# A second nested product in the setup, and three outer differences made by ScalarE and adding DMAs

## The chip, the cores and the metric

The kernel runs on one core of one Trainium2 chip. The metric is the device time of one execution in microseconds (us). The core has TensorE (PE: matmul, with its weight loads shown apart as PEld), VectorE (DVE), ScalarE (ACT), GpSimd (POOL), and SyncE (SP), which here only issues DMAs. GpSimd issues DMAs too, the ones that add to what stands at their destination. Each engine takes its instructions in order, and waits on semaphores for those of others.

## The reference

All is float32. With x of shape 8 x 1024 x 1024, a context `memory` of 8 x 64 x 512, and D = 1024:

```python
memory_proj = jnp.einsum('bme,de->bmd', memory, W_mem)
scores = jnp.einsum('bnd,bmd->bnm', hidden_states, memory_proj) / jnp.sqrt(jnp.float32(D))
attn = jax.nn.softmax(scores, axis=-1)
memory_context = jnp.einsum('bnm,bmd->bnd', attn, memory_proj)
gate_input = jnp.concatenate([hidden_states, memory_context], axis=-1)
gate = jax.nn.sigmoid(jnp.einsum('bnf,df->bnd', gate_input, W_gate) + b_gate)
fused = hidden_states + gate * memory_context
return _rmsnorm(fused, norm_w)
```

The large part is x times the first half of W_gate, W1 (1024 x 1024), for 8192 rows. The second half, W2, meets the context through attention: the kernel computes `mp`, the projected memory (512 rows of 1024 for all batches), and `mg`, mp times W2, once in a setup, and then only multiplies attention rows with them.

## The kernel before

**Blocks.** x is worked through in 16 blocks of 512 rows. A block's product with W1 is a Strassen product in Winograd's form on two levels: seven outer products (order 1, 6, 7, 5, 4, 2, 3), each of seven inner products of two 128x128 by 128x256 matmul pairs. The outer right sides are W1's quarters or differences of them: `outer_b[5] = 7 - 1` (quarter numbers: 1 upper left, 7 upper right, 2 lower left, 3 lower right), `outer_b[6] = 3 - 5`, `outer_b[7] = 3 - 7` in place, and `outer_b[4] = 2 - 6`. Each is 128 partitions by 2,048 columns. `outer_sum` makes them on VectorE. For each outer product o, four `inner_sum`s (T1, T2, R12 in place, T4; 128x512 each) prepare the inner right sides. `inner_s` does the same for the left sides, from the transposed x, on GpSimd. Before the second outer product of block 0 the scores of block 0 are computed, into the PSUM banks "b" and "c", which the inner products kB and kC of the first outer product have used and which two VectorE adds (u<-u,kB and u<-u,kC) free.

**Setup.** mp is made by Strassen on W_mem. Then mg is made by one outer Strassen level with the quarters m11 to m22 of mp (left) and b11 to b22 of W2 (right): `mg_product` is one dense product of 16 matmul passes of 512 columns; `second_product` replaces one by seven smaller ones (28 passes of 256 columns), with left sums from `second_left` (VectorE) and right sums from `second_right` and `second_sum` (GpSimd). In before only the fifth product (s1 by t1) is nested; the sixth (s2 by t2), like the others, is dense. While TensorE runs through the setup, GpSimd makes W2's and W1's differences, and VectorE makes left sums, outer differences, the transposes of block 0's x (`transpose_x`) and its outer left sums (`outer_s`).

**Order.** The order on every engine is the program's own: `pin` keeps each instruction in the order in which it is written. Buffers are shared by tag: `const` tags t4, t5, t6 hold W1's outer differences 4, 5, 6, and before that W2's t1 (t6) and t2 (t4); it1 to it7 hold the inner sums; it4 first holds the rows of mp that `first_rows` stores. `load_xq(q)` loads a block's x, 2 MB, in four DMAs from SP into the one buffer `xq`, when the transposes of the block ahead are done. After the setup a list of due times (`at`, by slots of one inner product) places the rest of the work between the products.

Of the kernel before, what the change touches and what calls it, by code (L numbers as in the profile page):

```python
# [15 lines left out]
P = 128  # L16
# [4 lines left out]
def tile_gated_cross_attention_rmsnorm(  # L21
# [73 lines left out]
    def tt(eng, o, a, b, op):  # L95
        pin(eng.tensor_tensor(o, a, b, op))  # L96
# [112 lines left out]
    pt += [bank("c", [P, BM], "pt3")]  # L209


    def outer_sum(o, a, b, k=slice(0, 4)):
        tt(nc.vector, outer_b[o][:, k], outer_b[a][:, k], outer_b[b][:, k], ALU.subtract)

    def inner_sum(eng, o, n):
        s, a, b = ((T1, R12, R11), (T2, R22, T1), (R12, R22, R12), (T4, R21, T2))[n]
        tt(eng, w_op(o, s), w_op(o, a), w_op(o, b), ALU.subtract)

    def inner_sums(eng, o):
        w1_place(o)  # L220
        for n in range(4):
            inner_sum(eng, o, n)
# [94 lines left out]
    def w2_sum(eng, o, a, b):  # L317
        for k in range(KH):
            tt(eng, o[k], a[k], b[k], ALU.subtract)

    def second_right(r, tag):
# [4 lines left out]
        return r11, r21, r12, r22, *(t[:, i, :, :] for i in range(3))  # L326

    def second_sum(eng, right, n):
        r11, r21, r12, r22, t4, t1, t2 = right
        o, a, b = ((t1, r12, r11), (t2, r22, t1), (t4, r21, t2), (r12, r22, r12))[n]  # L330
        tt(eng, o, a, b, ALU.subtract)

    right5 = second_right(t_w2[0], "it3")
    for k in range(KH):
        tt(nc.gpsimd if k > 1 else nc.vector, t1[k], b12[k], b11[k], ALU.subtract)
    for n in range(3):
        second_sum(nc.gpsimd, right5, n)
    w2_sum(nc.gpsimd, t2, b22, t1)
    second_sum(nc.gpsimd, right5, 3)
    pm_sum(m22, m22, up)  # L340
    outer_sum(5, 7, 1)
    w2_sum(nc.gpsimd, b12, b22, b12)
    inner_sums(nc.gpsimd, 1)

    pm_product(both, ps4, e22)
    pm_copy(m21, both)
    pm_product(up, pw22, e21)
    pm_copy(m12, up)


    A, S, L2, O = {}, {}, {}, {}
# [4 lines left out]
    def transpose_x(q, t, half):  # L356

        key = q, t // 2, half
        if key not in A:
            A[key] = t4k(  # L360
                apool, [P, KH, 2 * P], f"a{t // 2 + 1}{half + 1}", f"a{t // 2 + 1}{half + 1}_{q}"
            )
        r = t % 2
        pin(
            nc.vector.transpose(  # L365
                A[key][:, :, r * P : (r + 1) * P],
                chunks(xq[q][:, 4 * t : 4 * t + 4, :], KD)[:, half * KH : (half + 1) * KH],
            )
        )
# [167 lines left out]
    def store_mpT(r, h):  # L537
        load(mpd[:, h * KH : (h + 1) * KH, r * HM : (r + 1) * HM], mpT[r][h])
# [22 lines left out]

    def first_rows():

        t = const.tile([P, 2, Q4], F32, tag="it4", name="rows0")
# [22 lines left out]
    def second_left(eng, l, tag):  # L587

        l11, l12, l21, l22 = quarters(l)
        t = const.tile([P, 5, 2, P], F32, tag=tag, name="mg_left")  # L590
        s1, s2, s3, s4, zs = (t[:, i, :, :] for i in range(5))
        tt(eng, s1, l21, l22, ALU.add)
        tt(eng, s2, s1, l11, ALU.subtract)
        tt(eng, s3, l11, l21, ALU.subtract)
        tt(eng, s4, l12, s2, ALU.subtract)
        return l11, l12, l22, s1, s2, s3, s4, zs.rearrange("p k c -> p (k c)")

    def second_product(left, right, pgs, between):

        l11, l12, l22, s1, s2, s3, s4, zs = left  # L600
        r11, r21, r12, r22, t4, t1, t2 = right
        top, low = pgs
        u2 = bank("b", [P, C], "mg_u2")
        z = u3 = bank("c", [P, C], "mg_u3")

        def product(o, l, r, start=False):
            for k in range(2):
                mm(o, l[:, k, :], r[:, k, :], start and k == 0, k == 1)
# [15 lines left out]
        product(top[:, C:H], s4, r22)  # L624
        between()
        product(low[:, 0:C], l22, t4)
        tt(nc.vector, low[:, C:H], low[:, C:H], zs, ALU.add)

    def mg_tile(pool, tag, name):
        return t4k(pool, [P, 2, H], tag, name)  # L630

    def mg_copy(o, pgs):
        for t in range(2):
            pin(nc.scalar.copy(o[t] if isinstance(o, list) else o[:, t, :], pgs[t]))
# [5 lines left out]
        )  # L640

    s1 = mp_step(nc.vector, "s1", apool, m21, m22, ALU.add)
    store_mpT(0, 1)
    load_xq(0)
    c11 = mg_tile(rot, "u", "mg_c11")
    c12 = mg_tile(rot, "u", "mg_c12")
    c21 = mg_tile(rot, "l2", "mg_c21")
    c22 = mg_tile(small, "mg", "mg_c22")
    up, side = side, up
    mg_product(m11, b11, up, True)  # L650
    mg_copy(both, up)
    left5 = second_left(nc.vector, s1, "it6")

    def left6():
        nonlocal s2
        s2 = mp_step(nc.vector, "s2", apool, s1, m11, ALU.subtract)

    s2 = None
    second_product(left5, right5, side, left6)
    mg_copy(c22, side)  # L660
    outer_sum(7, 3, 7)
    w1_place(7)
    for n in range(4):
        inner_sum(nc.gpsimd, 7, n)
    mg_product(m12, b21, up)
    mg_copy(c11, up)
    store_mg(c11, 0, 0)
    first_rows()
    load_mp(0)
    s3 = mp_step(nc.vector, "junk", small, m11, m21, ALU.subtract)  # L670
# [36 lines left out]
    outer_s(0, 2)  # L707
    load_mg(0)


# [484 lines left out]
```

## Time and profile before

| | |
|---|---|
| median of 3 runs | 945.4 us (945.01 to 946.05) |
| the profiled execution's own time | 944.76 us |
| its span, first to last instruction | 943.0 us |
| TensorE busy | 932.1 us (99%) |
| VectorE, GpSimd, ScalarE busy | 801.6, 736.8, 432.5 us |
| granted TensorE clock | 0.997 |
| setup's mg products on TensorE | from 31.5 us to 78.8 us |
| x loads, 512 KB each, issue to landing, median | 9.9 us |
| GpSimd's adding DMAs, 512 KB each, issue to landing, median | 8.3 us |

A row of the timeline gives start, duration, engine, line, operation, output tile <- input tiles, shapes, count, and in brackets the idle time before it with what ended it. Nearly all matmuls go through one helper (line 93) and nearly all two-input sums through another (line 96), so rows are told apart by tile names: t_w is W2's t1 or t2, w a buffer of W1 or W2, t an outer difference, it an inner sum, l inner left sums, mg_u the small PSUM banks of the nested product, pm_af, pm_ed and pm_ctx the large ones, psT_b and psT_c the scores. A DMA row gives the size of one and the median time from its issue to its landing.

### The profile page before, as it was taken

To read this page: it belongs to the slowest core of one execution; us is meant where nothing else is said; L and a number is where in the kernel's file an instruction comes from. 1 tells how busy PE (TensorE), PEld (TensorE's weight loads), DVE (VectorE), ACT (ScalarE), POOL (GpSimd) and SP (SyncE) were. 2 spreads that over 40 slices of the span, in tenths; PEclk is the share of its full clock that TensorE was granted. 3 is DMA by queue.
4 is the path that set the end of the run, shared out by engine and by line. 5 is a ranking of instruction groups with operands and counts; after the bars stand their busy time and mean duration, and the time that the engine had idled before them with its cause. 6 is when DMAs were issued, how large, how long until landed. Compare 5 with 4: busy or idle time off the path is not lost.

```text
span 943.0 us, 15920 instructions
## 1 busy us (share of the span) xinstructions
PE 932.1 (99%) x5572; PEld 727.8 (77%) x5572; DVE 801.6 (85%) x1267; ACT 432.5 (46%) x1111; POOL 736.8 (78%) x814
## 2 busy tenths in 40 slices
PE   9999999999999999999999999999999999999995
PEld 8646778787877778787877778687877778787774
DVE  6799888888898888888897888888897889888887
ACT  4212336273644537263644527263643627264556
POOL 4998978689586868788586868778596868878695
PEclk9999999999999999999999999999999999999998
DMA  9927294582919365581919365491918466391632
GB/s 378 309 70 157 44 169 111 131 173 55 203 57 187 104 135 124 121 181 46 212 57 179 95 143 132 101 202 34 222 58 169 100 136 144 94 205 29 137 152 90
DMA packets 71184, 128.44 MB, mean 136 GB/s; under 512 B 12608, under 2 KB 49472, under 8 KB 70848
## 3 DMA queue, kind: packets, MB, share of 16 engines
q1 hardware_dynamic: 61920, 93.86, 38.1%
q0 software_dynamic: 9184, 33.56, 19.6%
q8 instruction: 45, 0.74, 0.3%
q14 instruction: 35, 0.29, 0.1%
HBM read 87.56 MB, written 41.68 MB: 137 GB/s over the span
## 4 chain that ended last, share of the span: by engine, by line
PE 96%; POOL 1%; DVE 1%; DMA 1%; ACT 0%; issue 0%; SPq 0%; POOLq 0%; ACTq 0%
PE af L93 32%; PE ed L93 21%; PE kC L93 10%; PE kB L93 10%; PE pc L93 10%; PE psT_af L93 5%; PE pm_ctx L93 3%; PE pm_af L93 2%; PE pm_ed L93 2%; DVE gate L96 1%; POOL gate L96 1%; DMA wm<-in_w_mem_t 1%; PE psT_ed L93 0%; PE mg_u L93 0%; PE psT_b L93 0%; POOL l L96 0%
## 5 line engine op out<-in xcount | busy, mean ns | idle before, releaser
L96 POOL TENSOR_TENSOR gate<-gate,u 128x512 f32<-128x512 f32 (+1 forms) x224 | 244.9, 1108 | 151.8 <-DVE u L96 150.8
L793 ACT ACTIVATE gate<-gate 128x512 f32<-128x512 f32 x127 | 80.0, 630 | 182.1 <-DVE gate L96 180.5
L365 DVE STREAM_TRANSPOSE a<-xq 128x512 f32<-128x512 f32 x128 | 141.9, 1112 | 8.9 <-PE af L93 8.0
L96 POOL TENSOR_TENSOR l<-a 128x256 f32<-128x256 f32 x128 | 112.9, 882 | 17.3 <-PE af L93 15.9
L93 PE MATMUL pc<-mg,attnT 64*64 64x512 f32 x512 | 117.0, 596 | 0.0
L93 PE MATMUL ed<-it,l 128*128 128x256 f32 x448 | 115.0, 379 | 0.0
L93 PE MATMUL kB<-it,l 128*128 128x256 f32 x448 | 115.0, 379 | 0.0
L822 DVE SCALAR_TENSOR_TENSOR gate<-gate,ss,nw_sb 128x512 f32<-128x512 f32 x120 | 109.7, 915 | 1.1
L93 PE MATMUL af<-w,a 128*128 128x256 f32 x384 | 98.5, 379 | 0.0
L1047 ACT COPY u<-af 128x256 f32<-128x256 f32 x112 | 41.4, 370 | 123.3 <-PE af L93 113.6
L96 DVE TENSOR_TENSOR gate<-gate,pc 128x512 f32<-128x512 f32 x128 | 85.5, 677 | 11.8 <-ACT gate L793 11.8
L93 PEld LDWEIGHTS ed<-it,l 128*128 128x128 f32 x448 | 85.1, 190 | 11.6
L93 PEld LDWEIGHTS kB<-it,l 128*128 128x128 f32 x448 | 85.1, 190 | 11.6
L96 DVE TENSOR_TENSOR gate<-gate,ed 128x512 f32<-128x512 f32 x112 | 76.3, 682 | 17.7 <-POOL gate L96 15.6
L96 DVE TENSOR_TENSOR gate<-gate,af 128x512 f32<-128x512 f32 (+1 forms) x128 | 76.0, 604 | 13.2 <-PE af L93 10.5
L96 POOL TENSOR_TENSOR l<-s 128x256 f32<-128x256 f32 x96 | 84.3, 878 | 1.2 <-issue 1.2
L93 PEld LDWEIGHTS af<-w,a 128*128 128x128 f32 x384 | 73.0, 190 | 10.3 <-issue 0.5
L93 PEld LDWEIGHTS pc<-mg,attnT 64*64 64x64 f32 x512 | 32.8, 132 | 49.6 <-issue 23.2
L93 PE MATMUL ed<-it,a 128*128 128x256 f32 x256 | 67.4, 386 | 0.0
L93 PE MATMUL af<-mg,attnT 64*64 64x512 f32 (+1 forms) x380 | 67.0, 457 | 0.0
L96 DVE TENSOR_TENSOR u<-u,kB 128x256 f32<-128x256 f32 x112 | 46.0, 410 | 24.7 <-PE kB L93 23.7
L93 PE MATMUL af<-t,s 128*128 128x256 f32 x256 | 65.8, 379 | 0.0
(213 smaller groups left out, 2129.2 us busy)
## 6 DMA issues: line engine op xcount, KB each, us to landing
xq<-in_x SPq DMA_DIRECT2D x64, 512.0 KB, 9.9
gate<-in_x POOLq DMA_DIRECT2D x60, 512.0 KB, 8.3
out<-gate SPq DMA_DIRECT2D x60, 512.0 KB, 3.0
w<-in_w_gate_t SPq DMA_DIRECT2D x8, 512.0 KB, 10.2
w<-in_w_gate_t SPq DMA_DIRECT2D x2, 2048.0 KB, 17.0
mg<-mgd SPq DMA_DIRECT2D x16, 256.0 KB, 4.8
wm<-in_w_mem_t SPq DMA_DIRECT2D x4, 512.0 KB, 6.0
mpd<-mpT SPq DMA_DIRECT2D x4, 512.0 KB, 9.5
```

The costliest lines, as they stand in the source:

```text
L93: pin(nc.tensor.matmul(o, lhsT, rhs, start=start, stop=stop, skip_group_check=True))
L96: pin(eng.tensor_tensor(o, a, b, op))
L365: nc.vector.transpose(A[key][:, :, r * P : (r + 1) * P], chunks(xq[q][:, 4 * t : 4 * t + 4, :], KD)[:, half * KH : (half + 1) * KH],)
L793: pin(nc.scalar.activation(g, g, AF.Sigmoid))
L822: nc.vector.scalar_tensor_tensor(g[:, cols], g[:, cols], rstd[:, t % 2 : t % 2 + 1], nw_sb[:, cols], ALU.mult, ALU.mult,)
L1047: pin(nc.scalar.copy(p1, af[:, 0]))
```

## The change

It has three parts.

- The sixth product is nested as well (`left6`, `right6`, `sums6`). It needs four more 128x512 sums on GpSimd, four more 128x256 sums on VectorE, and runs right behind the fifth, ahead of m12 by b21. Its third right sum goes to a spare buffer (tag it4) instead of in place, so that t2 stays whole. The first product, P1, is now kept in SBUF (`c21`) and added onto the sixth by two VectorE adds. b21 - t2 goes to b11's place.
- `outer_b[7]`, `outer_b[6]` and `outer_b[4]` are no longer VectorE's differences: ScalarE writes the negative of one operand (7, 5, 6), and a DMA issued by GpSimd adds the other (W1's lower right quarter, again that, and its lower left quarter, 1 MB each) from DRAM.
- The order follows: inner sums of 5 and 7 stand together on GpSimd behind the DMA for 6; `m12 - s2` moves from GpSimd to VectorE; VectorE's two inner sums of 4 stand behind `outer_s(0, 2)` instead of ahead of it.

```diff
-    def outer_sum(o, a, b, k=slice(0, 4)):
-        tt(nc.vector, outer_b[o][:, k], outer_b[a][:, k], outer_b[b][:, k], ALU.subtract)
+    def outer_sum(o, a, b):
+        tt(nc.vector, outer_b[o], outer_b[a], outer_b[b], ALU.subtract)
+
+    def outer_negative(o, b):
+        pin(nc.scalar.activation(outer_b[o], outer_b[b], AF.Copy, scale=-1.0))
+
+    def outer_add(o, h, c):
+        rows = rows_by_chunk(w_gate_t[:D, :], KD)[:, 4 * h : 4 * h + 4, c * H : (c + 1) * H]
+        pin(nc.gpsimd.dma_start(outer_b[o], rows, accum_op=ALU.add))
...
+    spare = const.tile([P, 3, 2, C], F32, tag="it4", name="spare")
+    right5, sums5 = second_right(t_w2[0], "it3")
+    right6, sums6 = second_right(t_w2[1], "it2", spare[:, 1, :, :])
     for k in range(KH):
         tt(nc.gpsimd if k > 1 else nc.vector, t1[k], b12[k], b11[k], ALU.subtract)
-    for n in range(3):
-        second_sum(nc.gpsimd, right5, n)
-    w2_sum(nc.gpsimd, t2, b22, t1)
-    second_sum(nc.gpsimd, right5, 3)
+    second_sums(nc.gpsimd, sums5[:3])
     pm_sum(m22, m22, up)
-    outer_sum(5, 7, 1)
-    w2_sum(nc.gpsimd, b12, b22, b12)
-    inner_sums(nc.gpsimd, 1)
-
     pm_product(both, ps4, e22)
     pm_copy(m21, both)
+    outer_sum(5, 7, 1)
     pm_product(up, pw22, e21)
     pm_copy(m12, up)
+    outer_negative(7, 7)
+    w2_sum(nc.gpsimd, t2, b22, t1)
+    second_sums(nc.gpsimd, sums5[3:])
+    second_sums(nc.gpsimd, sums6)
+    w2_sum(nc.gpsimd, b12, b22, b12)
+    outer_add(7, 1, 1)
+    inner_sums(nc.gpsimd, 1)
...
     s1 = mp_step(nc.vector, "s1", apool, m21, m22, ALU.add)
+    s2 = mp_step(nc.vector, "s2", apool, s1, m11, ALU.subtract)
...
     mg_product(m11, b11, up, True)
-    mg_copy(both, up)
-    left5 = second_left(nc.vector, s1, "it6")
...
-    second_product(left5, right5, side, left6)
+    mg_copy(c21, up)
+    left_sums5(0, 1, 2, 3)
+    left_sums6(0)
+    second_product(left5, right5, side, lambda: left_sums6(1))
+    left_sums6(2, 3)
...
+    second_product(left6, right6, both, left7)
     mg_copy(c22, side)
-    outer_sum(7, 3, 7)
-    w1_place(7)
-    for n in range(4):
-        inner_sum(nc.gpsimd, 7, n)
+    w1_place(6)
+    outer_negative(6, 5)
+    for t in range(2):
+        tt(nc.vector, both[t], c21[:, t, :], both[t], ALU.add)
+    mg_copy(c21, both)
+    w2_sum(nc.vector, b11, b21, t2)
+    outer_add(6, 1, 1)
+    for o in (5, 7):
+        if o == 7:
+            w1_place(o)
+        for n in range(4):
+            inner_sum(nc.gpsimd, o, n)
     mg_product(m12, b21, up)
     mg_copy(c11, up)
...
+    tt(nc.vector, s2, m12, s2, ALU.subtract)
     for part in range(2):
         inner_s(0, 1, part)
-    w2_sum(nc.vector, b21, b21, t2)
-    mg_product(s2, t2, both)
-    mg_copy(c21, both)
-    tt(nc.gpsimd, s2, m12, s2, ALU.subtract)
     for t in range(2):
         tt(nc.vector, side[t], c21[:, t, :], side[t], ALU.add)
-    w1_place(6)
-    outer_sum(6, 3, 5)
+    w1_place(4)
+    outer_negative(4, 6)
+    outer_add(4, 1, 0)
     for n in range(4):
-        inner_sum(nc.gpsimd, 5, n)
+        inner_sum(nc.gpsimd, 6, n)
     mg_product(s3, b12, both)
...
-    w1_place(4)
-    outer_sum(4, 2, 6)
-    for n in range(4):
-        inner_sum(nc.gpsimd, 6, n)
...
-    mg_product(m22, b21, both)
+    mg_product(m22, b11, both)
...
     load_xq(1)
     outer_s(0, 1)
-    for n in range(2):
-        inner_sum(nc.vector, 4, n)
     mg_product(s2, b22, side)
     mg_copy(c12, side)
     store_mg(c12, 0, 1)
     outer_s(0, 2)
+    for n in range(2):
+        inner_sum(nc.vector, 4, n)
     load_mg(0)
```

More of the change, by code (lines that the diff above doesn't have):

```diff
@@ L319, in w2_sum, with second_right @@
             tt(eng, o[k], a[k], b[k], ALU.subtract)
-    def second_right(r, tag):
+    def second_right(r, tag, t3=None):
         r11, r21 = (r[:, 2 * k : 2 * k + 2, 0:C] for k in range(2))
@@ L325, in second_right, with second_sums @@
         t = const.tile([P, 3, 2, C], F32, tag=tag, name="mg_right")
[L326 to L333, printed above, removed]
+        t1, t2, t4 = (t[:, i, :, :] for i in range(3))
+        t3 = r12 if t3 is None else t3
+        sums = (t1, r12, r11), (t2, r22, t1), (t4, r21, t2), (t3, r22, r12)
+        return (r11, r21, t3, r22, t4, t1, t2), sums
+    def second_sums(eng, sums):
+        for o, a, b in sums:
+            tt(eng, o, a, b, ALU.subtract)
+    spare = const.tile([P, 3, 2, C], F32, tag="it4", name="spare")
+    right5, sums5 = second_right(t_w2[0], "it3")
+    right6, sums6 = second_right(t_w2[1], "it2", spare[:, 1, :, :])
     for k in range(KH):
         tt(nc.gpsimd if k > 1 else nc.vector, t1[k], b12[k], b11[k], ALU.subtract)
-    for n in range(3):
-        second_sum(nc.gpsimd, right5, n)
-    w2_sum(nc.gpsimd, t2, b22, t1)
-    second_sum(nc.gpsimd, right5, 3)
+    second_sums(nc.gpsimd, sums5[:3])
     pm_sum(m22, m22, up)
-    outer_sum(5, 7, 1)
-    w2_sum(nc.gpsimd, b12, b22, b12)
-    inner_sums(nc.gpsimd, 1)
     pm_product(both, ps4, e22)
     pm_copy(m21, both)
+    outer_sum(5, 7, 1)
     pm_product(up, pw22, e21)
     pm_copy(m12, up)
+    outer_negative(7, 7)
[5 more added lines that the diff above has]
+    inner_sums(nc.gpsimd, 1)
     A, S, L2, O = {}, {}, {}, {}
@@ L562, in first_rows @@
     def first_rows():
-        t = const.tile([P, 2, Q4], F32, tag="it4", name="rows0")
+        t = spare[:, 0, :, :]
         for h in range(2):
@@ L585, in mg_product, with second_left, sums @@
                 mm(pgs[t], l[:, k, t * P : (t + 1) * P], r[k], start and k == 0, k == KH - 1)
-    def second_left(eng, l, tag):
+    def second_left(l, t, zs):
         l11, l12, l21, l22 = quarters(l)
[L590 to L596, printed above, removed]
+        s1, s2, s3, s4 = (t[:, i, :, :] for i in range(4))
+        def sums(*which):
+            for n in which:
+                o, a, b, op = (
+                    (s1, l21, l22, ALU.add),
+                    (s2, s1, l11, ALU.subtract),
+                    (s3, l11, l21, ALU.subtract),
+                    (s4, l12, s2, ALU.subtract),
+                )[n]
+                tt(nc.vector, o, a, b, op)
+        return (l11, l12, l22, s1, s2, s3, s4, zs), sums
     def second_product(left, right, pgs, between):
@@ L642, in tile_gated_cross_attention_rmsnorm @@
     s1 = mp_step(nc.vector, "s1", apool, m21, m22, ALU.add)
+    s2 = mp_step(nc.vector, "s2", apool, s1, m11, ALU.subtract)
     store_mpT(0, 1)
     load_xq(0)
+    lt5 = const.tile([P, 5, 2, P], F32, tag="it6", name="mg_left5")
+    lt6 = t4k(rot, [P, 4, 2, P], "l2", "mg_left6")
+    left5, left_sums5 = second_left(s1, lt5, lt5[:, 4, :, :].rearrange("p k c -> p (k c)"))
+    left6, left_sums6 = second_left(s2, lt6, spare[:, 2, 0, :])
     c11 = mg_tile(rot, "u", "mg_c11")
@@ L650, in tile_gated_cross_attention_rmsnorm, with left7 @@
     mg_product(m11, b11, up, True)
-    mg_copy(both, up)
-    left5 = second_left(nc.vector, s1, "it6")
[L654 to L658, printed above, removed]
-    second_product(left5, right5, side, left6)
-    mg_copy(c22, side)
-    outer_sum(7, 3, 7)
-    w1_place(7)
-    for n in range(4):
-        inner_sum(nc.gpsimd, 7, n)
+    mg_copy(c21, up)
[3 more added lines that the diff above has]
+    left_sums6(2, 3)
+    s3 = None
+    def left7():
+        nonlocal s3
+        s3 = mp_step(nc.vector, "junk", small, m11, m21, ALU.subtract)
+    second_product(left6, right6, both, left7)
+    mg_copy(c22, side)
+    w1_place(6)
[10 more added lines that the diff above has]
+            inner_sum(nc.gpsimd, o, n)
     mg_product(m12, b21, up)
```

1 line of the change is left out of this document (removed).

## The prediction

> **What bounds the kernel now.** I read the page first: which engine fills the span, and what the chain that ended last runs over.
>
> ```profile
> span 943.0 us, 15920 instructions
> PE 932.1 (99%) x5572; PEld 727.8 (77%) x5572; DVE 801.6 (85%) x1267; ACT 432.5 (46%) x1111; POOL 736.8 (78%) x814
> PE 96%; POOL 1%; DVE 1%; DMA 1%; ACT 0%; issue 0%; SPq 0%; POOLq 0%; ACTq 0%
> ```
>
> TensorE is the bound from end to end: a microsecond of matmul taken away is a microsecond gained, and a microsecond in which TensorE waits is never made up. So I read TensorE's timeline over the setup (start, duration, operation, tiles, count):
>
> ```profile
> 38.39 1.03 PE L93 MATMUL mg_u<-t_w,mp_s 128*128 128x256 f32 x4
> ...
> 44.50 3.60 PE L93 MATMUL pm_af<-w,mpT 128*128 128x512 f32 x8
> ...
> 51.37 7.03 PE L93 MATMUL pm_ctx<-t_w,mp_s 128*128 128x512 f32 x16
> 58.23 7.03 PE L93 MATMUL pm_ctx<-w,mp_junk 128*128 128x512 f32 x16
> ...
> 80.56 1.03 PE L93 MATMUL kC<-w,l 128*128 128x256 f32 x4
> ...
> 84.97 0.43 PE L93 MATMUL psT_b<-a,mpb 64*64 64x256 f32 x2
> ...
> 90.42 1.03 PE L93 MATMUL kC<-t,l 128*128 128x256 f32 x4
> ```
>
> 38.39 to 44.50 is the fifth product, nested already; 51.37 to 58.23 the sixth, dense. At 84.97 the first block's scores start, in the PSUM banks of kB and kC.
>
> **The gain.** The dense sixth product takes 58.23 - 51.37 = 6.86 us, the nested one 44.50 - 38.39 = 6.11 us (it should be 7/8 of 6.86, or 6.00; 0.11 us are its own small waits). I take 0.75 us; 0.86 us is the most, since nothing else leaves TensorE.
>
> **Does the nested product get its operands?** It now begins where the fifth ends, at 44.50. GpSimd's rows give the price of its sums:
>
> ```profile
> 31.45 6.46 POOL L96 TENSOR_TENSOR t_w<-w,t_w 128x512 f32<-128x512 f32 x4
> ...
> 39.28 5.92 POOL L96 TENSOR_TENSOR w<-w,w 128x512 f32<-128x512 f32 x4
> ...
> 59.43 1.17 POOL L96 TENSOR_TENSOR l<-a 128x256 f32<-128x256 f32 x1
> 60.67 0.72 POOL L96 TENSOR_TENSOR l<-l,a 128x256 f32<-128x256 f32 x1
> ...
> 71.71 1.27 POOL L96 TENSOR_TENSOR t<-t 128x512 f32<-128x512 f32 x1
> 72.95 1.27 POOL L96 TENSOR_TENSOR it<-t,it 128x512 f32<-128x512 f32 x1
> ```
>
> Undisturbed, a 128x512 sum on GpSimd begins 72.95 - 71.71 = 1.24 us after the one ahead. Where VectorE too runs sums with two SBUF inputs, it takes longer by about their time. The four sums for the sixth product begin where b12's began, at 39.28, plus the 1.3 us of VectorE's work that moves ahead of them (s2 and one left sum, 1,280 columns at about 1 us per thousand): 40.6. Four of them and two left sums between (0.3 us each) end at 46.2. The last, T3, is read by the fifth of seven matmul pairs, at 44.50 + 4 x 0.87 = 48.0. 1.8 us of cover: no cost; bounds 0 and 0.9 us, the sums being late by half as much again. On VectorE, s2 and left6's first sum come ahead of the fifth product's add:
>
> ```profile
> 30.28 2.29 DVE L96 TENSOR_TENSOR mp_s<-mpT,mpT 128x1024 f32<-128x1024 f32 x1
> ...
> 36.71 1.48 DVE L96 TENSOR_TENSOR mg_left<-mp_s,mg_left 128x256 f32<-128x256 f32 x1
> 42.12 0.43 DVE L96 TENSOR_TENSOR pm_af<-mg_u,mg_left 128x256 f32<-128x256 f32 x1 [3.92 <-PE pm_af L93]
> ...
> 61.13 2.42 DVE L96 TENSOR_TENSOR t<-w,t 128x2048 f32<-128x2048 f32 x1
> ...
> 72.17 2.12 DVE L365 STREAM_TRANSPOSE a<-xq 128x512 f32<-128x512 f32 x2 [0.87 <-PE pm_ctx L93]
> 76.44 1.75 DVE L96 TENSOR_TENSOR it<-t 128x512 f32<-128x512 f32 x1
> ...
> 82.01 0.41 DVE L96 TENSOR_TENSOR u<-u,kB 128x256 f32<-128x256 f32 x1
> 82.52 0.42 DVE L96 TENSOR_TENSOR u<-u,kC 128x256 f32<-128x256 f32 x1
> 82.86 0.68 DVE L96 TENSOR_TENSOR it<-w 128x512 f32<-128x512 f32 x1
> ...
> 89.09 0.42 DVE L96 TENSOR_TENSOR sT<-sT,psT_c 128x256 f32<-128x256 f32 x1 [0.58 <-ACT sT L429]
> ```
>
> 36.71 + 1.48 + 2.29 + 1.4 = 41.9, and the add is wanted at 42.12: it fits, by 0.2 us; cost 0, at most 0.3. Three outer sums like that of 2.42 us leave VectorE: no gain by itself, for VectorE isn't the bound. ScalarE's three negatives (2,048 columns each) I price from its rows:
>
> ```profile
> L793 ACT ACTIVATE gate<-gate 128x512 f32<-128x512 f32 x127 | 80.0, 630 | 182.1 <-DVE gate L96 180.5
> L807 ACT ACTIVATE junk<-gate 128x1024 f32<-128x1024 f32 x60 | 63.2, 1054 | 1.3
> ```
>
> 424 ns per 512 columns, so 1.9 us each; in the setup ScalarE mostly waits for TensorE. Cost 0, bounds 0 and 0.6 us (a PSUM copy behind a negative). The other added pieces (left sums, two adds of P1 in place of a copy) fall into idle stretches like the 3.92 us before 42.12.
>
> **Where a wait appears.** Outer quarter 4 is now made by a chain over four queues: GpSimd issues the adding DMA for 6; it lands; ScalarE negates 6 into 4; GpSimd issues the adding DMA for 4; it lands; VectorE takes two inner sums of 4. These two stand just ahead of u<-u,kB and u<-u,kC in VectorE's order, and the scores need the banks that those two adds free. Queued behind the waiting sum are thus VectorE's whole work on the first block, and TensorE.
>
> When is the last DMA issued? In before GpSimd reaches the block's first left sum at 59.43, after 17 sums of 512 columns from 31.45 on. After, 25 stand ahead: t2, T3 of product 5, four of product 6, b12, and the inner sums of 1, 5 and 7. VectorE's competing two-input columns in that stretch are 7,168 in both: before, four left sums, s2, outer 7, s3, b21; after, s2, eight left sums, s3, b11, s2 again. So 59.43 + 8 x 1.24 = 69.35, plus two DMA issues (0.9 us each in the rows below) 71.2, plus four left sums at 0.72: **74.0**. Bounds: 72.2 (issues that cost GpSimd nothing) and 75.1 (outer_s(0, 1), 1,024 columns, gets in between).
>
> What else is on the DMA engines then? The second block's x, 2 MB from SP in four loads. Issues and times to landing, of before, with two pairs of adding DMAs from later blocks:
>
> ```profile
> 74.31 1.99 SPq L99 DMA_DIRECT2D xq<-in_x  x4
> xq<-in_x SPq DMA_DIRECT2D x1, 512.0 KB, 5.6
> xq<-in_x SPq DMA_DIRECT2D x1, 512.0 KB, 7.9
> xq<-in_x SPq DMA_DIRECT2D x1, 512.0 KB, 12.1
> 176.45 0.88 POOL L797 DMA_DIRECT2D gate<-in_x  x1
> 177.03 1.20 POOL L797 DMA_DIRECT2D gate<-in_x  x1
> gate<-in_x POOLq DMA_DIRECT2D x1, 512.0 KB, 7.6
> 185.26 2.73 SPq L99 DMA_DIRECT2D xq<-in_x  x4
> 192.87 0.88 POOL L797 DMA_DIRECT2D gate<-in_x  x1
> gate<-in_x POOLq DMA_DIRECT2D x1, 512.0 KB, 13.4
> q1 hardware_dynamic: 788, 0.79, 115.3%
> q0 software_dynamic: 288, 1.05, 63.8%
> ```
>
> The landing rows are those of SP's first, second and fourth load (issued at 74.31, 74.70, 75.81) and of the second of each GpSimd pair. A pair is 1 MB, as much as one new DMA. With the engines free it lands 177.03 + 7.6 - 176.45 = 8.2 us after its start; behind the x load of 185.26 the second half alone takes 13.4 us. The last two rows are packets: from 193.5 to 197.5 only SP's queue moved (788 packets, none of GpSimd's, though issued); from 197.5 to 206.3 GpSimd's 1.05 MB did, at a mean of 200 GB/s in all, or 5.2 us per MB. Whoever is in line first goes first.
>
> The x load is tied to TensorE (its buffer is free after the transposes of 72.17), so it moves up by the gain: 73.6 to 75.1, against 74.0 for the adding DMA. The two arrive together. Worked through: nothing ahead, 74.0 + 8.2 = 82.2; one load ahead (landed at 74.31 + 5.6 - 0.75 = 79.2), plus 5.2: 84.4; two (74.70 + 7.9 - 0.75 = 81.85): 87.0; all four (75.81 + 12.1 - 0.75 = 87.2): 92.4. By issue times one to three are ahead; I take **87.0**.
>
> The Trainium skill, "DMA: Bandwidth & Descriptors", section "Queues, rings and completion order", has each engine round-robin between queues packet by packet; the row of 788 packets speaks against it here.
>
> From landing to scores: two inner sums at 0.68 and two adds at 0.41 and 0.42 make 2.2 us; scores at 89.2 in place of 84.97 - 0.75 = 84.2: TensorE stands for **5.0 us**. Then kC of the next product (90.42 - 84.97 = 5.45 us after the scores' start, so 94.7) waits for the add at 89.09, which ends 7.5 us after the first u add, 95.9 when that starts at 88.4; free of GpSimd's competition VectorE needs less. I take 0.4, between 0 and 1.2.
>
> Sum: -0.75 + 5.0 + 0.4 = **+4.65 us**. On the profiled execution 943.0 becomes 947.6 (its own time 944.8 becomes 949.4); it ran 0.6 us below the median shown, so for a median 945.4 + 4.65 = 950.0.
>
> **Rivals.** *The DMA gets ahead of x (not slower).* If GpSimd is a microsecond earlier than I count, or SP's loads are slow to fill the engines, it lands at 82.2 or before: scores at 84.4 or on time, -0.75 to -0.5, so 944.7 to 944.9; behind one load, at 84.4, the net is +1.8 to +2.0. It decides from a landing before 84.3. For it: 74.0 and 73.6 are closer than my bounds. Against it: SP is first by the count. *Round-robin.* 1 MB at half of 200 GB/s takes 5.2 us longer than 8.2 and lands at 87.4 whichever is first: +5.0, 950.4. This is the page's rule named above; only its chance differs, against it the 788 packets. *All four loads ahead.* Landing 92.4, scores at 94.6, 10.4 - 0.75 + 0.4 = +10.0: 955.4; for it, GpSimd's upper bound 75.1. *The change doesn't shorten the sixth product* (its small operands late): +0.9 - 0.75, about 945.6; against it the 1.8 us of cover.
>
> **How the numbers follow.** Forecast, one to three loads ahead (+2 to +8): 0.36; ahead of x: 0.34; all four: 0.12; round-robin: 0.07; product without gain: 0.06; something faster that I don't see: 0.02; others slower 0.03. The range 944.4 to 955.5 goes from the whole gain without any wait to all four loads ahead; the forecast's own is 947.4 to 953.4. About 0.2%, 1.9 us, is what a measurement of this kernel tells from no change. Faster by that is more than TensorE's 0.86 us: 0.02. Same: the 0.34 and the 0.06, and a little of the forecast's lower end: 0.42. Slower: the rest, 0.56.
>
> **What would show it.** Right: VectorE idle ahead of the first it<-t by some 7 us, released by the DMA into t; psT_b's first matmul near 89; GpSimd's third adding DMA issued within a microsecond of x's first load. Wrong: that DMA landing before 82, psT_b at 84.2; a gap within 44.5 to 50.6; or 25 sums done well before 71.

## The result, and the profile after

The changed kernel takes 950.48 us (median of 6 runs, 950.35 to 951.64); before took 945.4 us beside it (944.73 to 946.35). The ratio is 1.0056, 95% interval [1.0043, 1.0069]: slower by about 5 us, as forecast. But the trace shows that most of these 5 us are lost in another place than the one forecast.

The profiled execution took 950.37 us (its span, first to last instruction, is 948.6 us). Its view of waits (in us: total, times, longest), rows of TensorE:

```profile
PE pm_ctx L93 <- DVE mg_c L96: 4.2, 1, 4.2
PE pz L93 <- DVE zeros L116: 1.2, 1, 1.2
```

These are all rows of TensorE's waits in that view. The second stands in before too; the first is new, and the forecast wait (psT_b for u) isn't there. TensorE's timeline shows where it lies:

```profile
44.50 1.03 PE L93 MATMUL mg_u<-t_w,mp_s 128*128 128x256 f32 x4
...
50.61 3.60 PE L93 MATMUL pm_af<-w,mpT 128*128 128x512 f32 x8
...
57.48 7.03 PE L93 MATMUL pm_ctx<-w,mp_junk 128*128 128x512 f32 x16
68.73 8.83 PE L93 MATMUL pm_ctx<-w,mpT 128*128 128x512 f32 x16 [4.23 <-DVE mg_c L96]
77.40 3.60 PE L93 MATMUL pm_af<-w,mp_s 128*128 128x512 f32 x8
...
84.27 1.03 PE L93 MATMUL af<-w,a 128*128 128x256 f32 x4
...
90.40 0.43 PE L93 MATMUL psT_b<-a,mpb 64*64 64x256 f32 x2
```

and in before, where block 0 starts:

```profile
78.83 1.03 PE L93 MATMUL af<-w,a 128*128 128x256 f32 x4
```

The nested sixth product runs from 44.50 to 50.61 without a gap: 6.11 us. After s3·b12 (from 57.48, done at about 64.35) TensorE stands until 68.73. It waits to start m22·b11, which goes into the PSUM banks that s3·b12 filled, and those are free only when VectorE has added them to c22. The product itself then takes 77.40 - 68.73 = 8.67 us in place of 6.87. Block 0 starts at 84.27, 5.44 us later than the 78.83 of before: -0.75 (nested product) + 4.38 (from 64.35 to 68.73) + 1.80 (slow product) = 5.43. The rest of the program loses only 0.2 us more (the span is 5.6 us longer).

Nearly all of the 1.80 us are the clock. The windows of the changed kernel give, for each stretch, PE, PEld, DVE, ACT and POOL busy, then the granted clock, the DMA share and GB/s. They are cut at the edges of the stretch at half clock:

```profile
63.05:66.46 3.41, 1.46 (x4) 0.38 (x2) 3.41 (x3) 0.00 (x0) 3.41 (x4) 1.00 1.11 204
66.46:69.87 3.41, 1.14 (x3) 0.66 (x4) 3.41 (x6) 1.02 (x1) 3.33 (x3) 1.00 0.90 198
69.87:73.28 3.41, 3.41 (x5) 1.35 (x5) 1.47 (x2) 0.89 (x1) 3.33 (x5) 0.50 0.41 154
73.28:76.69 3.41, 3.41 (x9) 1.48 (x8) 0.00 (x0) 0.59 (x1) 3.41 (x5) 1.00 0.03 3
```

Behind the wait the granted clock stands at half for 3.41 us (69.87 to 73.28). 3.41 us at half speed cost 1.7 us.

Why is VectorE late? Its timeline, changed kernel:

```profile
51.22 1.28 DVE L96 TENSOR_TENSOR pm_ctx<-mg_c,pm_ctx 128x512 f32<-128x512 f32 x2
52.41 7.58 DVE L96 TENSOR_TENSOR w<-w,t_w 128x512 f32<-128x512 f32 x4
...
60.86 4.00 DVE L377 STREAM_TRANSPOSE a<-xq 128x512 f32<-128x512 f32 x4
64.79 2.09 DVE L96 TENSOR_TENSOR mp_s<-mpT,mp_s 128x1024 f32<-128x1024 f32 x1
66.81 0.68 DVE L96 TENSOR_TENSOR pm_af<-mg_c,pm_af 128x512 f32<-128x512 f32 x1
67.41 0.68 DVE L96 TENSOR_TENSOR pm_ed<-mg_c,pm_ed 128x512 f32<-128x512 f32 x1
68.00 1.27 DVE L96 TENSOR_TENSOR mg_c<-mg_c,pm_ctx 128x512 f32<-128x512 f32 x2
...
77.60 2.12 DVE L377 STREAM_TRANSPOSE a<-xq 128x512 f32<-128x512 f32 x2 [6.26 <-PE pm_ctx L93]
...
85.61 0.69 DVE L96 TENSOR_TENSOR it<-t 128x512 f32<-128x512 f32 x1
```

and the answering rows of before:

```profile
53.68 6.33 DVE L96 TENSOR_TENSOR w<-w,t_w 128x512 f32<-128x512 f32 x4
...
63.47 0.68 DVE L96 TENSOR_TENSOR mg_c<-mg_c,pm_ctx 128x512 f32<-128x512 f32 x1
65.30 0.69 DVE L96 TENSOR_TENSOR mg_c<-mg_c,pm_ctx 128x512 f32<-128x512 f32 x1 [1.16 <-PE pm_ctx L93]
65.91 3.37 DVE L96 TENSOR_TENSOR t<-w,t 128x2048 f32<-128x2048 f32 x1
```

In before VectorE is ahead of TensorE here: it waits 1.16 us for the product, and then has time for outer quarter 4 (65.91 to 69.28). In the changed kernel VectorE has no idle time from 51.22 to 71.3 and reaches the c22 adds at 68.00. Ahead of them stand the two adds of P1 (1.28, new), four sums for b11 that take 7.58 us in place of the 6.33 of b21's in before, the transposes, which before were done ahead of its sums for b21 (53.68), and m12 - s2 (2.09, moved here from GpSimd). Not all of the lateness is added work: from 42.5 to 51.2 VectorE also stood for the nested product's matmuls, 1.67, 1.08 and 0.30 us, against 0.69 us in before, because nothing else stands there in its order. The last transposes (77.60) overwrite m22's buffer and so wait for m22·b11, and the load of the second block's x for them, so the wait moves that load too. The issues of the changed kernel's GpSimd and SP, and the DMA's landing:

```profile
74.63 1.27 POOL L220 DMA_DIRECT2D t<-in_w_gate_t  x1
79.75 3.52 SPq L99 DMA_DIRECT2D xq<-in_x  x4
t<-in_w_gate_t POOLq DMA_DIRECT2D x1, 1024.0 KB, 9.1
```

The third adding DMA goes out at 74.63, five microseconds ahead of x, and lands 9.1 us later, at 83.75. x's first packets come at about 82, when all but 0.07 MB of its 1 MB has moved, so it is as good as alone. VectorE, itself late, comes to the inner sums of 4 at 85.61 and finds it there. The forecast collision was hidden behind the wait that I had not seen.

### The profile page after: what moved, and what is told of

Read it like the earlier page. It is cut to its first block, busy times and chain, and to the rows that moved or that the text cites. A ratio compares the mean times of both kernels' runs of the same rounds, so it can differ in the third digit from the quotient of the medians.

```text
span 948.6 us, 15976 instructions
## 1 busy us (share of the span) xinstructions
PE 933.4 (98%) x5584; PEld 730.5 (77%) x5584; DVE 802.5 (85%) x1273; ACT 439.2 (46%) x1118; POOL 737.2 (78%) x820
## 4 chain that ended last, share of the span: by engine, by line
PE 94%; DVE 3%; POOL 1%; issue 1%; ACT 0%; POOLq 0%; DVEq 0%; ACTq 0%
PE af L93 31%; PE ed L93 21%; PE kB L93 10%; PE kC L93 10%; PE pc L93 10%; PE psT_af L93 5%; PE pm_ctx L93 2%; PE pm_af L93 2%; PE pm_ed L93 2%; DVE gate L96 1%; POOL gate L96 1%; PE mg_u L93 1%; DVE w L96 1%; PE psT_ed L93 0%; PE pz L93 0%
## 5 line engine op out<-in xcount | busy, mean ns | idle before, releaser
L96 POOL TENSOR_TENSOR l<-a 128x256 f32<-128x256 f32 x128 | 109.8, 858 | 18.9 <-PE af L93 15.9
L96 DVE TENSOR_TENSOR gate<-gate,ed 128x512 f32<-128x512 f32 x112 | 76.3, 682 | 17.6 <-POOL gate L96 15.6
L96 POOL TENSOR_TENSOR l<-s 128x256 f32<-128x256 f32 x96 | 83.8, 873 | 4.8 <-ACT u L1074 4.8
L93 PEld LDWEIGHTS af<-w,a 128*128 128x128 f32 x384 | 73.0, 190 | 10.3 <-issue 0.5
```

The lines of the kernel that those rows point to most:

```text
L93: pin(nc.tensor.matmul(o, lhsT, rhs, start=start, stop=stop, skip_group_check=True))
```

## The experiments

Two theories. A: the changed kernel loses its time to VectorE's lateness at the c22 adds (4.4 us, and the clock 1.8 us), so moving these adds gains about 6 us. B, my prediction's: the third DMA collides with the x load. If B is real but hidden, removing A's wait must bring it out. All kernels below are edits of the changed one, called e1, e2 and so on as in the recorded expectations; before took 945.5 to 945.9 us beside them. Each has one trace, of one of its runs. Some profiles start the setup's mg products up to 1.1 us later than the 31.53 us of before; the edits do not touch what stands there, and single profiles are longer by so much.

**The c22 adds first (e1).** The third product (s3 by b12) and its adds are moved ahead of half the transposes.

```diff
-    for t in range(4):
+    for t in range(2):
         transpose_x(0, t, 0)
+    mg_product(s3, b12, both)
+    for t in range(2):
+        tt(nc.vector, c22[:, t, :], c22[:, t, :], both[t], ALU.add)
+    store_mg(c22, 1, 1)
+    for t in (2, 3):
         transpose_x(0, t, 0)
     tt(nc.vector, s2, m12, s2, ALU.subtract)
...
-    mg_product(s3, b12, both)
-    for t in range(2):
-        tt(nc.vector, c22[:, t, :], c22[:, t, :], both[t], ALU.add)
-    store_mg(c22, 1, 1)
```

> The two adds c22 += both (and the third product's place in the program with them) stand ahead of two of the four transposes, of m12 - s2 and of the side adds in VectorE's order. Theory A, the loss is TensorE's wait for the bank `both` ahead of m22 by b11 and the half clock behind it: that wait goes (third product's end at 64.4 us, next matmul at 64.4), the clock stays 1.00, block 0 starts near 78.1. Theory B, the one on record (the third adding DMA and the x load collide, VectorE's first inner sum of 4 waits): the x load moves back to about 74.5 us, against 74.6 for the DMA, so the collision that the changed kernel escaped is back; landing 83.7 if the DMA is in line first (scores at 86, net +1.1 us against the kernel before, 946.5), 85 to 92 if behind one to four x loads (net +2.5 to +10, 948 to 955). If A alone holds and this DMA costs nothing: 944.7.

Measured: 955.36 us, ratio 1.0095 [1.0082, 1.0108], slower still. TensorE in this kernel:

```profile
64.59 7.03 PE L93 MATMUL pm_ctx<-w,mpT 128*128 128x512 f32 x16
...
93.56 1.12 PE L93 MATMUL psT_b<-a,mpb 64*64 64x256 f32 x4 [9.03 <-DVE u L96]
```

VectorE, at the first inner sum of 4:

```profile
91.75 0.69 DVE L96 TENSOR_TENSOR it<-t 128x512 f32<-128x512 f32 x1 [12.00 <-DMA t<-in_w_gate_t]
```

The window behind the start of the wait (columns as above):

```profile
86.90:96.70 9.80, 3.14 (x28) 2.35 (x32) 4.77 (x7) 0.00 (x0) 3.45 (x2) 0.50 0.73 189
```

The issues, of SP's timeline and GpSimd's:

```profile
73.92 1.93 SPq L99 DMA_DIRECT2D xq<-in_x  x4
...
76.08 1.29 POOL L220 DMA_DIRECT2D t<-in_w_gate_t  x1
```

The queues' packets, MB and share, from 76.5 to 83 (first row; q1 is SP's, q0 GpSimd's) and from 84 to 90:

```profile
q1 hardware_dynamic: 1355, 1.35, 114.2%
...
q0 software_dynamic: 439, 0.90, 80.7%
q1 hardware_dynamic: 438, 0.47, 30.2%
```

The bank wait is gone (m22·b11 follows at 64.59), so A's place is right, but taking the wait away gained nothing, for B comes out: x now goes out at 73.92, 2.16 us ahead of the DMA, which lands at 91.68, 15.6 us after its issue. VectorE waits 12.00 us for it and TensorE 9.03, and the clock is at half for 10.24 us, from 86.70 to 96.94: two thirds of that lie in the wait and cost nothing, the 3.4 us from 93.56 on cost 1.7 us. The packets show how the DMA is held up: to 83 only SP's queue moves; GpSimd's first packets come at about 83.8, 7.7 us after the issue; from 84 to 90 both queues move, 439 packets to 438.

**The same, and the third DMA early (e2).** The negative and the DMA for 4 go ahead of the first inner left sums.

```diff
+    w1_place(4)
+    outer_negative(4, 6)
+    outer_add(4, 1, 0)
     for part in range(2):
         inner_s(0, 1, part)
...
-    w1_place(4)
-    outer_negative(4, 6)
-    outer_add(4, 1, 0)
```

> As e1_c22_early, and the adding DMA for outer quarter 4 is issued ahead of GpSimd's four inner left sums of block 0 instead of behind them, about 2.8 us earlier (near 71.8 us), well ahead of the x load. Theory A and B agree: the DMA lands near 81 us, VectorE's inner sums of 4 find it there, scores start near 84.2, no wait is left and only the 0.75 us of the nested product remain: 944.7, a little under the kernel before. If it stays at 946 or more, something else in the change costs (left sums too late for kB, or a wait that neither theory has).

Measured: 949.1 us (947.01 to 950.35), 1.0029 [1.0018, 1.0041]. VectorE's row in its profile (own time 947.01):

```profile
82.21 1.43 DVE L96 TENSOR_TENSOR it<-t 128x512 f32<-128x512 f32 x1 [2.70 <-DMA t<-in_w_gate_t]
```

TensorE, at the scores (it waits 0.62 us more at the next kC):

```profile
85.15 0.65 PE L93 MATMUL psT_b<-a,mpb 64*64 64x256 f32 x4 [0.86 <-DVE u L96]
```

Issued at 71.81, three microseconds ahead of x, the DMA lands at 82.13. The one thing changed is when that DMA and the negative ahead of it are issued, and it takes 6 us off: the wait behind the late DMA is B's, and it is shown. But landing takes 10.3 us, and VectorE still waits, so the 944.7 of a DMA in time were not reached. The trace is that of the run of 947.01 us; what four of the other five took beyond it, 1.7 to 3.3 us, no trace shows.

**Only m12 - s2 moved (e4).** In the changed kernel, this one line goes behind the c22 adds; the third product stays in its place.

```diff
-    tt(nc.vector, s2, m12, s2, ALU.subtract)
...
     store_mg(c22, 1, 1)
+    tt(nc.vector, s2, m12, s2, ALU.subtract)
```

> The changed kernel with one instruction moved: m12 - s2 (128x1024 on VectorE) stands behind the two adds c22 += both instead of ahead of them. Theory A: the adds and TensorE's wait end 2.1 us earlier (wait 2.2 us instead of 4.2); if a wait of that length leaves the clock at 1.00, the 1.7 us of half clock go too: 950.4 - 2.1 - 1.7 = 946.6; if the clock still falls, 948.3. Theory B: no change in what counts, the DMA for 4 lands where it did, 950.4.

Measured: 950.17 us, 1.0046 [1.0034, 1.0058]: nothing gained on the changed kernel. TensorE:

```profile
67.79 7.13 PE L93 MATMUL pm_ctx<-w,mpT 128*128 128x512 f32 x16 [2.19 <-DVE mg_c L96]
...
90.10 0.65 PE L93 MATMUL psT_b<-a,mpb 64*64 64x256 f32 x4 [2.26 <-DVE u L96]
```

The first wait falls by 2 us, and the clock stays whole behind it (the product takes 6.97 us). But x comes earlier by as much (77.09), the DMA of 75.73 shares with it and lands at 88.22, and the second wait takes 2.3 us and a stretch at half clock. (This run took 952.23 us. Three of the other four, of 949.2 to 950.2 us, have a granted clock of 0.997 or 0.998 against 0.995 here, which speaks against such a stretch in them.) What the first wait loses in length the second gains, because x moves with the first.

**Work for TensorE in the wait (e3, e7).** Four more matmuls of 512 columns, whose product nothing uses, are put into the wait; nothing else is changed. In e3 their left side is m11. I had overlooked that the transposes of x overwrite its buffer.

```diff
+    fill = bank("b", [P, H], "fill")
+    for k in range(KH):
+        mm(fill, m11[:, k, 0:P], b22[k], k == 0, k == KH - 1)
     mg_product(m22, b11, both)
```

> The changed kernel with four more 512-column matmuls (m11 by b22, used by nobody, in the free bank b) between the third product and m22 by b11; nothing else differs. They fill 3.4 of the 4.2 us in which TensorE waits. If the slow matmuls behind the wait (8.67 us for the product in place of 6.87) come from the clock that the idle time lowered, the granted clock stays 1.00, the product takes 6.87 again and the time falls by 1.7 to 1.8 us: 948.7. If they come from something else (the DMAs or VectorE beside them), the time stays at 950.4.

Measured: 957.55 us, 1.0119 [1.0105, 1.0134]. VectorE's transposes waited for the filler, and the c22 adds with them. VectorE in this kernel:

```profile
68.67 4.07 DVE L377 STREAM_TRANSPOSE a<-xq 128x512 f32<-128x512 f32 x4 [6.85 <-PE fill L93]
```

and TensorE:

```profile
76.02 9.87 PE L93 MATMUL pm_ctx<-w,mpT 128*128 128x512 f32 x16 [7.40 <-DVE mg_c L96]
```

In e7 the left side is m22, whose buffer is overwritten only behind m22·b11:

```diff
-        mm(fill, m11[:, k, 0:P], b22[k], k == 0, k == KH - 1)
+        mm(fill, m22[:, k, 0:P], b22[k], k == 0, k == KH - 1)
```

> The changed kernel with four unused matmuls of m22 by b22 (512 columns, into the free bank b) in TensorE's wait ahead of m22 by b11. Unlike e3_filler's, whose left side m11 lies in the buffer that the first x transposes overwrite (they waited for the filler, 6.9 us), m22's buffer is overwritten only after m22 by b11. The filler should take 3.4 of the 4.2 us, the wait's end stay at 68.7, the granted clock stay at 1.00 and the product behind it take 6.87 us: 950.4 - 1.75 = 948.7. If the slow matmuls have another cause: 950.4.

Measured: 949.49 us, 1.0042 [1.0028, 1.0055]. That is 1.0 us less than the changed kernel; the two intervals overlap, so the trace has to say it. TensorE:

```profile
64.53 3.60 PE L93 MATMUL fill<-w,mpT 128*128 128x512 f32 x8
69.06 7.13 PE L93 MATMUL pm_ctx<-w,mpT 128*128 128x512 f32 x16 [0.93 <-DVE mg_c L96]
```

The banks come free no sooner (69.06, against 68.73), but the product takes 6.97 us in place of 8.67, and block 0 starts at 82.89 in place of 84.27. Behind useless work the granted clock stays at 1.00 in the trace: of the changed kernel's loss, 1.7 us are the clock.

**Does the wait come through VectorE's inner sums of 4 (e8)?** The first edit again, the DMA as late as there (75.48, with x at 75.55), but all four inner sums of 4 behind the thirteenth and fourteenth inner products.

```diff
     outer_s(0, 2)
-    for n in range(2):
-        inner_sum(nc.vector, 4, n)
...
+    for n in (0, 1):
+        at(13, inner_sum, nc.vector, 4, n)
     for n in (2, 3):
-        at(4, inner_sum, nc.gpsimd, 4, n)
+        at(14, inner_sum, nc.gpsimd, 4, n)
```

> e1_c22_early with nothing moved but the consumers of the adding DMA for 4: VectorE's two inner sums of 4 go from ahead of the first block's u adds to nine products later (slot 13, near 93 us), GpSimd's two to slot 14. Issue of that DMA and of the x load stay, so it should still land near 84 to 92 us. If e1's 9.0 us wait ahead of the scores is what the record says (VectorE stands for the DMA with the u adds behind it), the wait is gone wholly, the clock stays at 1.00, and with the nested product's 0.75 us the time is 944.7 to 945.0. If the DMA traffic itself slows TensorE or the others, some of the 9 us stays: 947 or more.

Measured: 948.42 us, 1.0035 [1.0022, 1.0047]: 7 us under the version with the sums in their place, though its DMA lands at 89.26. The 9.03 us and the half clock are gone; what stood behind the waiting sum, not the DMA itself, was the cost. TensorE now waits for GpSimd's left sums instead, which is most of what still parts it from before:

```profile
PE af L93 <- POOL l L96: 2.2, 1, 2.2
```

**Other ways to the same end (e6, e10, e12).** In e6 the early DMA of e2, with VectorE's two sums behind the third inner product:

```diff
     outer_s(0, 2)
-    for n in range(2):
-        inner_sum(nc.vector, 4, n)
...
+    for n in (0, 1):
+        at(3, inner_sum, nc.vector, 4, n)
```

> e2_c22_and_dma_early with VectorE's two inner sums of 4 behind the u adds (slot 3) instead of ahead of them. e2 still waited 0.9 us ahead of the scores and 0.6 us ahead of kC, and its runs spread from 947.0 to 950.4. If the wait for the DMA (landing near 82 us) explains both, the spread closes and the time is 944.7 to 945.2; if it stays near 947 to 949, e2's remainder lies elsewhere.

Measured: 949.2 us, 1.0032 [1.002, 1.0045]. The profile (949.23 us) starts the setup's mg products 0.94 us late, and the DMA goes out at 72.92, only 1.7 us ahead of x. It landed at 85.00 and the sums, now behind the u adds, waited 2.85 us for it, and kC for what was behind them:

```profile
93.09 1.37 PE L93 MATMUL kC<-t,l 128*128 128x256 f32 x4 [2.33 <-DVE sT L96]
```

In e10 the first edit (e1) with outer 4 as VectorE's subtraction again, so that there is no third DMA:

```diff
-    outer_negative(4, 6)
-    outer_add(4, 1, 0)
+    outer_sum(4, 2, 6)
```

> e1_c22_early with one of the three outer differences put back: 4 is VectorE's one subtraction again (2.2 us, behind the side adds) instead of ScalarE's negative and the third adding DMA. No DMA is left in the chain ahead of the block's u adds. If e1's loss of 10 us is this DMA's, it goes: VectorE is done with the two inner sums of 4 near 82 us, scores start near 84.2, time 944.7 to 945.2. If VectorE, with 2.2 us more, is now late itself, the scores wait about 1 us: 946.

Measured: 947.87 us, 1.0017 [1.0008, 1.0026]: 7.5 us less than with the DMA. VectorE, with the subtraction back, is itself late by a little: TensorE waits 0.96 us for it at the scores and 1.4 us at kC.

In e12 the first edit (e1) with the x load behind c12's store, so that x comes after the DMA:

```diff
-    load_xq(1)
     outer_s(0, 1)
...
     store_mg(c12, 0, 1)
+    load_xq(1)
```

> e1_c22_early with the second block's x load moved behind the store of c12 in SP's order (near 79 us instead of 73.9), so that the third adding DMA (issued near 76) is in line first; nothing else moves. If e1's landing at 91.7 us came from the x loads ahead of it, it lands about 9.1 us after its issue, near 85, as in the changed kernel; scores then start near 87.4 instead of 93.6, the wait falls from 9.0 to about 3 us and the clock's drop shrinks or goes: 947.5 to 949.5. If the DMA is slow by itself at that place (GpSimd or VectorE starving it), landing and time stay near 91.7 and 955.

Measured: 948.14 us, 1.0028 [1.0018, 1.0039]. Here the DMA of 76.60 goes out 3.5 us ahead of x, its first packets come about 2 us after the issue, and it lands 9.5 us after it, in place of 15.6, and the wait falls from 9.03 to 3.31 us:

```profile
88.37 0.65 PE L93 MATMUL psT_b<-a,mpb 64*64 64x256 f32 x4 [3.31 <-DVE u L96]
```

So the x load is worth 6 us of the landing, and the 9.5 us that are left are nearly what the DMA takes alone (9.1 in the changed kernel).

**Can the gain be had (e9, e11, e13)?** In e9 the early DMA of e2, with VectorE's sums behind the seventh inner product and GpSimd's behind the eighth:

```diff
     outer_s(0, 2)
-    for n in range(2):
-        inner_sum(nc.vector, 4, n)
...
+    for n in (0, 1):
+        at(7, inner_sum, nc.vector, 4, n)
     for n in (2, 3):
-        at(4, inner_sum, nc.gpsimd, 4, n)
+        at(8, inner_sum, nc.gpsimd, 4, n)
```

> e2_c22_and_dma_early with VectorE's two inner sums of 4 at slot 7 (near 88 us, where e8's VectorE stood idle for 1.3 us ahead of the scores' add) and GpSimd's two at slot 8, so that neither engine stands for the DMA (landing at 82 to 85 us) nor holds back other work as in e6 (kC waited 2.3 us) and e8 (a left sum came 2.2 us late). If the waits for this DMA and what they push are all that the change still costs once the bank wait is gone, TensorE waits nowhere and the time is the kernel before's less 0.75 us: 944.7 to 945.2. If 947 or more remains, something else is left.

Measured: 946.76 us, 1.0011 [1.0002, 1.0021]. In e11 all four on GpSimd, behind the fourth:

```diff
     outer_s(0, 2)
-    for n in range(2):
-        inner_sum(nc.vector, 4, n)
...
-    for n in (2, 3):
+    for n in range(4):
         at(4, inner_sum, nc.gpsimd, 4, n)
```

> e2_c22_and_dma_early with all four inner sums of 4 on GpSimd at slot 4, where e8's GpSimd stood idle for 3.9 us: VectorE no longer stands for the DMA at all, and GpSimd reaches them near 86 us, after the landing at 82 to 85. e9's remaining waits (1.3 us and twice 0.2, for GpSimd's left sums) came from sums put later. If these are the whole remainder of e9's +0.9 us, the time is 944.9 to 945.5, at or just under the kernel before; if it stays at 946.5 or more, the four sums on GpSimd push its left sums as far as e9's did.

Measured: 947.71 us, 1.002 [1.0012, 1.0029]. And in e13, from e9, all four on VectorE:

```diff
     for n in (2, 3):
-        at(8, inner_sum, nc.gpsimd, 4, n)
+        at(14, inner_sum, nc.vector, 4, n)
```

> The version with the third adding DMA early and VectorE's inner sums of 4 behind the seventh inner product, but with GpSimd's two inner sums of 4 given to VectorE too, behind the fourteenth. If the 1.3 us that the products of block 1 wait for GpSimd's inner left sums (af<-l) come from the two inner sums put among them, that wait goes, and what is left is the shorter sixth product: 946.8 - 1.3 = 945.5, no slower than before. If VectorE's own work in blocks 0 and 1 has no room for two more sums (it waits 2.3 us for GpSimd's gate adds in that stretch, two sums take 1.4), waits for u<-kB or u<-kC take its place: 946.5 to 947.5.

Measured: 946.65 us, 1.0011 [1.0002, 1.002]. None beats before, and the last says why. Its block 0 starts at 78.18, 0.65 us ahead of before (0.76 when the 0.11 us of a later start are counted): the setup has its whole gain. In block 1 TensorE then waits 1.30 us for GpSimd's left sums, although GpSimd has no inner sum of 4 any more. VectorE:

```profile
96.53 0.68 DVE L96 TENSOR_TENSOR t<-t 128x512 f32<-128x512 f32 x1
97.13 1.22 DVE L96 TENSOR_TENSOR it<-t,it 128x512 f32<-128x512 f32 x1
```

GpSimd, at the gate adds:

```profile
101.83 2.18 POOL L96 TENSOR_TENSOR gate<-gate,u 128x512 f32<-128x512 f32 x1 [1.76 <-DVE u L96]
```

TensorE:

```profile
106.37 1.10 PE L93 MATMUL af<-t,l 128*128 128x256 f32 x4 [1.30 <-POOL l L96]
```

In before that row of GpSimd stands at 100.27, behind a wait of 0.47 us, and TensorE does not wait. The sums on VectorE delay its u adds, GpSimd's gate adds wait for these, and the left sums stand behind the gate adds. The same wait is 1.3 us in all three versions, whichever engine takes the sums (on GpSimd alone kB waits 1.0 us more). I read it so: in the first two blocks neither engine has room for them, and a quarter that is ready at 82 to 85 us, where before had it at 69.28, puts them there. No run tried other slots in later blocks.

## Why the prediction was right, and where its reasons were not

The sign was right, and so was the time (950.0 forecast, 950.48 measured), but the time by luck: 5.4 us of waits at the scores and kC that the changed kernel doesn't have stand in the sum in place of 6.2 us of wait and clock at m22·b11 that it doesn't hold. One step of the working was missing, and the one that carried the sum was hidden in the kernel as changed.

- **The gain** (0.75 us): right. 6.11 us without a gap; in the last version the whole 0.76 us reach block 0.
- **The operands in time, the negatives for nothing**: right. ScalarE's negatives took 1.91 to 1.93 us (forecast 1.9) and TensorE waited for nothing behind them.
- **When the third DMA goes out** (74.0; bounds 72.2 to 75.1): 74.63; the first left sum at 71.79 (forecast 71.2).
- **"The other added pieces (left sums, two adds of P1 in place of a copy) fall into idle stretches like the 3.92 us before 42.12"**: the step that failed. That idle stretch lies ahead of the sixth product; the two adds of P1 come behind it, where VectorE has none. And m12 - s2 I counted only for what it takes from GpSimd, not in VectorE's own order. Both stand ahead of the c22 adds, which free the banks of m22·b11. From 51.22 on, 1.28 + 7.58 + 1.1 (the rows for the store) + 4.0 + 2.1 + 1.3 (the two adds onto `side`) puts those adds at 68.6 (68.00 in the trace, neighbours overlapping a little), against a product done at 64.35; with the 6.33 us that the rows of before gave for b21's sums it would have been 67.3, so the wait was there to be found. That wait, with the clock, costs 6.2 us.
- **x and the DMA arrive together** (x at 73.6 to 75.1): x came at 79.75, since it hangs on TensorE and TensorE stood. So VectorE had no gap ahead of its first inner sum of 4, psT_b came at 90.40 without a wait, and the DMA went out five microseconds ahead of x: nothing on the list of what would show me right was met, and nothing on the list of what would show me wrong either.
- **5.0 us of wait at the scores**: hidden, but real. With the first wait taken away it was 9.03 us, in place of the 5.0 that I chose; the DMA landed at 91.68, near the 92.4 of the rival "all four loads ahead". That is not its mechanism, though: both queues moved packets from 84 on.
- **"Whoever is in line first goes first"**: half right. In e1 the first 1,355 packets were SP's alone; after that both queues moved. The 788 packets of before showed the first half only. And the place in line is not the order of issue: in e8 the DMA, issued 0.07 us ahead of x, moved its first packets only at about 81.3, 5.8 us later.
- **The landing with nothing ahead** (8.2 us): too short. As good as alone it took 9.1 and 9.5 us here.
- **The clock behind a wait**: not priced, 1.7 us. The sum with the missed wait but a whole clock is 3.6 + 945.4 = 949.0, so the clock too had its part in the time's coming near the forecast.

Of the rivals, "the DMA gets ahead of x" is what the changed kernel does, but five microseconds ahead and for another reason than GpSimd being early, and the time that it gave (944.7) assumed that nothing else waits.

## What to carry to other kernels

When work is moved onto an engine, follow that engine's order on until it is idle again, and ask at every PSUM bank that it frees when the producer wants it back: an engine that was 1.16 us early can become 4 us late without being the bound anywhere else. A wait that is found may hide a second, because what it holds back (here the x load) would otherwise arrive in the way of something else; take it away before believing that it was the whole cost. And a sum that was free in the setup need not be free once its input comes so late that it must be done among the blocks.

## What the runs showed of the hardware

**A wait of TensorE can cost its clock too, and its length alone doesn't say whether.** Windows of the version with only m12 - s2 moved (e4), columns as above, around its waits of 2.19 and 2.26 us:

```profile
63.98:67.39 3.41, 1.62 (x4) 0.38 (x2) 3.41 (x5) 0.00 (x0) 3.41 (x4) 1.00 1.08 198
87.87:91.28 3.41, 1.18 (x16) 0.71 (x20) 2.85 (x5) 0.37 (x1) 2.21 (x2) 1.00 1.15 204
91.28:94.69 3.41, 3.41 (x38) 2.14 (x32) 3.38 (x6) 0.00 (x0) 1.23 (x1) 0.50 1.15 201
```

and of the version with x behind c12's store (e12):

```profile
83.43:86.84 3.41, 1.63 (x8) 1.10 (x6) 0.67 (x1) 0.37 (x1) 3.21 (x5) 1.00 1.06 301
86.84:90.26 3.42, 1.89 (x31) 1.18 (x35) 3.25 (x6) 0.00 (x0) 2.92 (x2) 1.00 1.16 190
90.26:93.67 3.41, 3.41 (x45) 2.39 (x38) 3.41 (x6) 0.37 (x1) 0.54 (x1) 1.00 1.15 202
```

A wait of 2.26 us brought a stretch at half clock; one of 2.19 us in the same trace brought none (the product behind it took 6.97 us), nor did one of 3.31 us. Every stretch at half clock around a wait was 3.41 us long or three times that (10.24 us, with waits of 9.03 and 7.40 us, and then it began within the wait). The stretches at full clock ahead of them were whole multiples of 3.41 us too: 19 in the changed kernel, 24 in e1, 25 in e4. It is as if the clock were set anew each 3.41 us by what TensorE did in the last 3.41. Cut into such windows over their whole span, all fourteen traces agree: each window at full clock in which TensorE was busy for 1.24 us or less was followed by one at half clock, and none in which it was busy for 1.46 us or more. So what counts is not a wait's length but how it falls: the first wait of e4 lies across the edge of two windows, with 1.62 and 3.01 us of work, and so does that of e12, with 1.63 and 1.89. The windows are not tied to the program's start: the first stretch at full clock starts between 4.2 and 6.8 us of the span in the fourteen traces, so by this reading the same wait can cost 1.7 us in one run and nothing in the next. No run moved a wait by itself against the windows.

The Trainium skill, "TensorE: Matmul & The Clock Gate", section "What's actually happening", has such a free-running window of 3413 ns and puts the drop behind an idle one. The length agrees; but here a window that was a third busy was followed by a drop.

**A late DMA first waits, then shares.** Behind the x load the adding DMA took 15.6 us to land (e1), as good as alone 9.1 to 9.5. In e1 GpSimd's queue moved nothing for 7.7 us after the issue. In e12, where only x's place differs, its first packets came after about 2 us with the same work on GpSimd and VectorE; and in e1 VectorE stood idle from 79.75 on. So it is x's load that held them back, and not those engines. By what means it did isn't settled by these runs.

The Trainium skill, "DMA: Bandwidth & Descriptors", section "Queues, rings and completion order", has the engines take turns between queues packet by packet. The 439 packets against 438 agree; the 1,355 of SP alone before them, with the DMA issued, don't.
